# Layer 1 of a state-space kernel on Trainium2: three groups of 64 channels, two states to a unit

## The chip, the cores and the metric

The kernel runs on one core of one Trainium2 (trn2) chip. The engines of a core run side by side and meet through semaphores: TensorE (PE in the profile; PEld is its weight load), VectorE (DVE), ScalarE (ACT), GpSimd (POOL) and SyncE (SP), whose queue issues nearly all of the kernel's DMA transfers. The metric is the device time of one execution in microseconds (us); the median of several runs counts.

## What is computed

The input x has 64 x 64 tokens of 96 channels. Two Mamba-like layers are applied in turn, each behind a group norm and with its input added at the end. Layer 0 scans the picture in four directions. Layer 1, which the change is about, scans the 4096 tokens once, in order, with 192 inner channels d and 16 states n. Cut to what matters:

```python
xc = silu(causal depthwise conv of 3 taps over the x half of W_in u)   # 192 channels
dt, Bm, Cm = split(xc @ W_x)                                           # 6 + 16 + 16
delta = softplus(dt @ W_dt + b_dt)                                     # called dt in the kernel
dA = exp(delta[..., None] * A);  dBu = delta[..., None] * Bm[:, :, None, :] * xc[..., None]
def step(h, inp):
    h = dA_t * h + dBu_t
    return h, einsum('bdn,bn->bd', h, C_t)
y = scan(step) + xc * D
out = (y * silu(z)) @ W_out
```

So for each of 192 x 16 pairs of channel and state there is one recurrence over 4096 tokens, and the 16 states of a channel are summed with C as weights.

## The kernel before

Every engine operation is recorded through one helper (`Ordered`, line 377 in the profile), which also fixes the order on each engine as the order in which the program writes the instructions. A tile's name (y, f, C, dA) therefore tells an instruction apart, and its line does not.

**Layout.** Tokens are taken in four chunks of 1024 columns. The 128 partitions hold channels 0 to 127; the other 64 channels stand in columns 1024 to 1535 of tiles of 1536 columns, the first 512 tokens in partitions 0 to 63, the next 512 in 64 to 127 (`half1`, `part`). u, sz, dt and w (dt times u) have this form.

**Units.** A chunk has 24 units. In units 0 to 15 the partitions are the 128 low channels with one state n. In units 16 to 23 they are the 64 high channels twice, with states n and n + 8 (`UNITS`, line 36). For units 16 to 23 dt and w are needed on both halves of the partitions with all 1024 columns: `front_dup` (line 1444) copies them by DMA into tiles dt1 and w1 (pool "dup", two buffers), eight transfers of 128 KB a chunk. `of_unit` (line 1457) picks the source.

**One unit s** goes through these steps:

- `load`: SP loads row n of C, spread over the partitions (one DMA of 512 KB, or two of 256 KB where the unit has two states). There are six C buffers. For the units of `POOL_UNITS` (five in each chunk) B is loaded in the same way, into one buffer.
- `spread`: otherwise PE spreads B over the partitions, into the PSUM tile f (two buffers): a matmul with a picking matrix, on B split in bfloat16 parts (`front_b`).
- `decay`: ACT computes dA = exp(dt * A). For POOL's units it goes to an f buffer, and POOL multiplies B by w (`pool_f`).
- `scan`: DVE multiplies f by w and runs the recurrence into h (three buffers); ACT keeps the last column (`keep_last`).
- `times_c`: POOL multiplies C by h.
- `fold`: PE adds the product to y: for units 0 to 15 with the identity into y0 (128 output columns, two banks), for 16 to 23 with the matrix `both` into y1 (64 output columns for each half of the tokens, one bank). The skip term u * D enters by `skip` with diagonal weights.

A matmul in float32 is two records in the trace, so a fold is four.

**Order.** `run` (line 1804) writes the steps by hand: in step s it issues the shared work of the chunk (`between`), the loads of unit s + 3, the spread and POOL's decay for s + 1, ACT's decay for s + 2, the softplus pieces, the scan of s, the product with C of s - 1 and the fold of s - 2. `between` puts the next chunk's projections, the output of the chunk before (`back`) and z between the units. `soft` (line 1767) spreads the next chunk's softplus over the steps from 10 on (15 in chunk 0): Abs, two sigmoids, two squares in a step each, DVE's two products in a step each, w on POOL, the copies. After unit 20 `gate(c, 0)` multiplies y0 by sz; `gate(c, 1)` for y1 comes with the next chunk. `start` (line 1686) does the front of chunk 0 and `end` the output of chunk 3.

Of the kernel before, what the change touches and what calls it, by code (L numbers as in the profile page):

```python
# [20 lines left out]
C = 96  # L21
# [18 lines left out]
WHOLE = 4  # L40

# [68 lines left out]
def minus_exp(nc, sb, vec, name):  # L110

    a = sb.tile([P, NVEC - ALOG], F32, name=f"A_{name}")
    nc.scalar.activation(a, vec[:, ALOG:], AF.Exp)
    nc.vector.tensor_scalar(a, a, -1.0, None, ALU.mult)
    return a
# [19 lines left out]
def load_layer1(nc, sb, vec, w_z, w_x, dt_w, w_out):  # L135

    lay = {}
    lay["vec"] = sb.tile([P, NVEC], F32, name="vec_1")
    nc.sync.dma_start(lay["vec"], vec)
    lay["w_z"] = sb.tile([C, 2, P], F32, name="wz_1")  # L140
    nc.sync.dma_start(lay["w_z"], w_z)
    lay["dt_w"] = sb.tile([DT_ROW + R, 2, P], F32, name="dtw_1")
    nc.sync.dma_start(lay["dt_w"][DT_ROW:], dt_w)
    lay["w_x"], lay["w_out"] = [], []
    for t in range(2):
        raw = sb.tile([P, E], F32, name=f"w_x_raw{t}")
        w_o = sb.tile([P, C], F32, name=f"w_out{t}_1")
        for to, src in ((raw, w_x), (w_o, w_out)):
            if t == 0:
                nc.sync.dma_start(to, src[0:P])  # L150
            else:
                nc.sync.dma_start(to[0:HALF], src[P:DI])
                nc.sync.dma_start(to[HALF:P], src[P:DI])
        wx = sb.tile([P, ROWS], F32, name=f"w_x{t}_1")
        nc.gpsimd.memset(wx, 0.0)
        for copy in range(3):
            nc.gpsimd.tensor_copy(wx[:, 32 * copy : 32 * copy + NS], raw[:, R : R + NS])
        nc.gpsimd.tensor_copy(wx[:, DT_ROW : DT_ROW + R], raw[:, 0:R])
        nc.gpsimd.tensor_copy(wx[:, C_ROW : C_ROW + NS], raw[:, R + NS : E])
        lay["w_x"].append(wx)  # L160
        lay["w_out"].append(w_o)
    return lay
# [1107 lines left out]
class Layer1:  # L1270
# [6 lines left out]
    def __init__(self, nc, tc, st, k, lay, w_in, conv_w, x1, stats, bc_dram, out, g):  # L1277
# [39 lines left out]
        for n, b in (("f", 2), ("y0", 1), ("y1", 1), ("misc", 1)):  # L1317
            self.pools[n] = st.enter_context(
                tc.tile_pool(name=f"{n}_1{g}", bufs=b, space=PSUM)
            )  # L1320
# [38 lines left out]

    def conv_taps(self, xn):  # L1360
        return [(self.cw[:, j, :], xn[:, j : j + CH]) for j in range(3)]

    def z_taps(self, xn):
        return [(self.lay["w_z"].rearrange("c t p -> c (t p)"), xn[:, 2 : 2 + CH])]
# [24 lines left out]
    def front_z(self, c):  # L1389
        of, self.at = self.chunks[c], c  # L1390
        of["sz"] = sz = self.tile("uz", [P, CW], "sz")
        for q in range(3):
            ps = self.misc(c, [P, NB], f"pz{q}")
            yield from self.steps(self.product(ps, q, self.z_taps(of["xn"])))
            self.nc.scalar.copy(sz[:, self.part(q)], ps)
# [48 lines left out]
    def front_dup(self, c):  # L1444

        of = self.chunks[c]
        self.at = c
        of["dup"] = {}
        for name in ("dt", "w"):
            of["dup"][name] = to = self.tile("dup", [P, CH], f"{name}1")  # L1450
            for share in range(2):
                for hf in range(2):
                    self.nc.sync.dma_start(
                        to[self.half1(share), self.part(hf)], of[name][self.half1(hf), CH:CW]
                    )

    def of_unit(self, name, s):
        c, i = divmod(s, UNIT)
        of = self.chunks[c]
        return of[name][:, 0:CH] if i < NS else of["dup"][name]  # L1460
# [31 lines left out]
    def load(self, s):  # L1492
        self.at, of = s, self.units[s]
        c, i = divmod(s, UNIT)
        for part, name in enumerate("BC"):
            if part or self.on_pool(s):
                of[name] = self.tile(name, [P, CH], name)
                load_states(
                    self.nc, of[name], self.bc_dram[part], 0, (UNITS[0] + UNITS[1])[i], c
                )  # L1500
# [10 lines left out]
    def spread(self, s):  # L1511
        self.at = s
        c, i = divmod(s, UNIT)
        self.units[s]["f"] = f = self.tile("f", [P, CH], "f")
        for hf in range(2):
            if s < WHOLE:
                pick, of = free(self.k["ident"][0:B_ROWS, :], (0, P), at=i), "dbl"
            else:
                pick, of = self.k["pick"][:, i, :], "B"
            self.nc.tensor.matmul(  # L1520
                f[:, self.part(hf)], pick, self.chunks[c][of][0:B_ROWS, self.part(hf)],
                start=True, stop=True,
            )
# [24 lines left out]
    def skip(self, c, q):  # L1548

        of, self.at = self.chunks[c], c  # L1550
        if q == 0:
            of["y0"] = self.tile("y0", [P, CH], "y0")
        if q == 2:
            of["y1"] = self.tile("y1", [P, NB], "y1")
        self.nc.tensor.matmul(
            of["y1"] if q == 2 else of["y0"][:, self.part(q)], self.diag[:, q // 2, :],
            of["u"][:, self.part(q)], start=True, stop=False,
        )

    def fold(self, s):  # L1560
        nc, k, terms = self.nc, self.k, self.units[s]["C"]
        c, i = divmod(s, UNIT)
        of = self.chunks[c]
        for hf in range(2):
            if i == 0:
                self.skip(c, hf)
            if i < NS:
                nc.tensor.matmul(
                    of["y0"][:, self.part(hf)], k["fold"][0], terms[:, self.part(hf)],
                    start=False, stop=(i == NS - 1),  # L1570
                )
            else:
                nc.tensor.matmul(
                    of["y1"][self.half1(hf), :], k["fold"][1][:, 0:HALF], terms[:, self.part(hf)],
                    start=False, stop=(i == UNIT - 1),
                )


    def gate(self, c, t):
        of, col = self.chunks[c], (slice(0, CH), slice(CH, CW))[t]  # L1580
        self.at = c
        if t == 0:
            of["v"] = self.tile("v", [P, CW], "v")
        self.nc.vector.tensor_mul(of["v"][:, col], of[f"y{t}"], of["sz"][:, col])

    def out_products(self, c, hf, po):
# [3 lines left out]
            ((po, w, of), {"start": i == 0, "stop": i == 2})  # L1590
            for i, (w, of) in enumerate((
                (self.k["ident"][0:C, 0:C], self.x1[:, cols]), (w_out[0], v[:, self.part(hf)]),
                (w_out[1][half, :], v[half, CH:CW]),
# [29 lines left out]
    def end(self):  # L1623
# [3 lines left out]
        at = self.tile("y0", [P, 2, NB], "y0")  # L1627
        po = [at[0:C, hf] for hf in range(2)]
        products = [self.out_products(c, hf, po[hf]) for hf in range(2)]
        for part in products:  # L1630
            for args, kw in part[0:2]:
                nc.tensor.matmul(*args, **kw)
        yield
        self.gate(c, 1)
        for part in products:
            args, kw = part[2]
            nc.tensor.matmul(*args, **kw)
# [17 lines left out]
    def start(self):  # L1655
# [55 lines left out]
        self.front_w(0, (slice(0, CH),), nc.vector)  # L1711
# [3 lines left out]
        pz, pz1 = bank("y0", [P, 2, NB], "pz"), bank("y1", [P, NB], "pz1")  # L1715
        for q in range(2):
            do(self.product(pz[:, q], q, self.z_taps(xn)))
        do(self.product(pz1, 2, self.z_taps(xn)))
# [7 lines left out]
        for q in range(3):  # L1726
            nc.scalar.copy(sz[:, self.part(q)], pz[:, q] if q < 2 else pz1)
# [10 lines left out]
    def between(self, c):  # L1738

        more = c + 1 < NSC  # L1740
        if c == 0:
            yield from self.front_u(1)
        yield from self.silus(c)
# [4 lines left out]
        if c:  # L1748
            self.gate(c - 1, 1)
        self.skip(c, 2)  # L1750
# [19 lines left out]
    def soft(self, c):  # L1770

        def piece(c, col):
# [7 lines left out]
            for i in range(2):  # L1780
                soft_square(nc, k, q, i)
                yield
            soft_times(nc, acc, q)
            yield
            nc.vector.scalar_tensor_tensor(dt, dt, 0.0, acc, ALU.max, ALU.add)
            yield
            self.front_w(c, (col,), nc.gpsimd)
            yield
            self.front_dup(c)
# [4 lines left out]
        for i in range(UNIT):  # L1794
# [4 lines left out]
            next(done, None)  # L1799
            if i in ((18, 20, 21, 22) if c == 0 else (14, 16, 18, 20)):  # L1800
# [3 lines left out]
    def run(self):  # L1804
# [5 lines left out]
        for s in range(n + 2):  # L1810
# [27 lines left out]
            if i == NS + 4 and c < NSC:  # L1838
                self.gate(c, 0)
# [10 lines left out]
def tile_kernel(  # L1850
# [44 lines left out]
    def load(nc):  # L1895
# [4 lines left out]
        lay0["A"] = minus_exp(nc, const, lay0["vec"], "0")  # L1900
# [10 lines left out]
        lay1["A"] = minus_exp(nc, const, lay1["vec"], "1")  # L1911

        k["pick"] = pick = const.tile([B_ROWS, NS + NS // 2, P], BF16, name="pick")
# [3 lines left out]
        for first, n, at, cols in (  # L1917
            (0, NS, 0, slice(0, P)),
            (0, NS // 2, NS, slice(0, HALF)),
            (NS // 2, NS // 2, NS, slice(HALF, P)),  # L1920
        ):
            nc.gpsimd.tensor_copy(
                pick[:, at : at + n, cols],
                free(state, (1, n), (0, cols.stop - cols.start), at=first),
            )
# [85 lines left out]
```

## Time and profile before

| | us |
|---|---|
| median of 3 runs | 570.2 |
| lowest and highest | 567.95, 571.04 |
| the profiled execution | 571.18 |
| its span, first to last instruction | 569.4 |
| busy PE | 482.6 |
| busy DVE | 461.7 |
| busy POOL | 348.8 |
| busy ACT | 328.4 |

The span is what the profile's times refer to; the profiled execution's own time is 1.8 us longer and 1.0 us above the median. Busy times are sums over the whole span, and the span has stages with different limits: layer 0 to about 158 us, the front of layer 1 to 187, the 96 units to 555, the tail. The chain of work that ended last goes through PE for 24% of the span and through DVE for 23%. "x96" is a number of instructions, and a row "a <-b" says that b ended the wait of a. PE's ends are modelled, so in PE's timeline the distance from one start to the next is more certain than a duration.

### The profile page before, as it was taken

The page shows a single profiled execution, that of the slowest core. Times are in us where ns is not written, and L with a number is a line of the kernel's source. Part 1 is how long each engine was busy: PE and PEld are TensorE (multiplying, and loading weights), DVE is VectorE, ACT ScalarE, POOL GpSimd, SP SyncE. Part 2 cuts the span into 40 slices and gives each one's busy share as a digit, 9 for nine tenths or more (in the row PEclk, how much of TensorE's full clock was granted, in tenths as well). Part 3 has the DMA queues.
Part 4 walks back from the last instruction along what each step waited for, and adds up shares of the span by engine and source line. Part 5 has one row for each costly group of instructions (what it writes and reads, how often), then busy time and mean ns, then how long its engine had stood idle before and what let it go on. Part 6 is the DMA issues. An engine that isn't in the chain of part 4 may idle for free.

```text
span 569.4 us, 4766 instructions
## 1 busy us (share of the span) xinstructions
PE 482.6 (85%) x1363; PEld 195.3 (34%) x1363; DVE 461.7 (81%) x442; ACT 328.4 (58%) x486; POOL 348.8 (61%) x204
## 2 busy tenths in 40 slices
PE   4999999988889998996899978679976847986782
PEld 3545445436732333331133323113422202432220
DVE  6897989255733979998989979896978899899991
ACT  5437993478636876695856765464585454243300
POOL 7080010014320697989997859975886988789861
PEclk9996999997997999997599979779989767999778
DMA  6103800000003537786655649764648675677701
GB/s 170 21 9 72 281 2 0 0 1 1 2 28 113 155 130 222 214 202 154 192 195 188 207 94 224 201 187 126 199 142 198 149 184 184 199 238 190 191 22 35
DMA packets 30502, 75.76 MB, mean 133 GB/s; under 512 B 10880, under 2 KB 12156, under 8 KB 30210
## 3 DMA queue, kind: packets, MB, share of 16 engines
q1 hardware_dynamic: 29186, 73.83, 45.8%
q10 hardware_dynamic: 1280, 1.52, 0.9%
q8 instruction: 13, 0.21, 0.2%
q14 instruction: 23, 0.19, 0.1%
HBM read 68.93 MB, written 2.25 MB: 125 GB/s over the span
## 4 chain that ended last, share of the span: by engine, by line
PE 24%; DVE 23%; ACT 11%; POOL 5%; issue 4%; DMA 4%; SPq 1%; POOLq 0%; DVEq 0%; ACTq 0%
DVE h L377 15%; PE y L377 11%; DVE f L377 5%; PE f L377 3%; ACT q L377 3%; POOL C L377 2%; PE pd L377 2%; ACT dA L377 2%; PE po L377 2%; DMA C<-bc_dram 2%; ACT f L377 2%; SPq L377 1%; PE pc L377 1%; ACT L377 1%; PE pv L377 1%
## 5 line engine op out<-in xcount | busy, mean ns | idle before, releaser
L377 POOL TENSOR_TENSOR C<-C,h 128x1024 f32<-128x1024 f32 x96 | 229.5, 2403 | 51.4 <-issue 19.6
L377 DVE TENSOR_TENSOR_SCAN h<-dA,last,f 128x1024 f32<-128x1024 f32 x57 | 133.8, 2347 | 7.9 <-POOL C L377 0.5
L377 PE MATMUL y<-C,ident 128*128 128x512 f32 x256 | 130.5, 632 | 4.5 <-POOL C L377 4.3
L377 DVE TENSOR_TENSOR f<-f,w 128x1024 f32<-128x1024 f32 x76 | 92.4, 1215 | 16.8 <-PE f L377 16.2
L377 ACT ACTIVATE dA<-dt,A 128x1024 f32<-128x1024 f32 x76 | 86.3, 1143 | 2.2 <-DVE h L377 1.9
L377 PE MATMUL f<-parts,pick 96*128 96x512 bf16 x144 | 50.5, 437 | 35.6 <-DVE h L377 35.6
L377 PEld LDWEIGHTS y<-C,ident 128*128 128x128 f32 x256 | 50.9, 203 | 60.5 <-issue 43.1
L377 PE MATMUL pc<-pad,cw 96*128 96x512 f32 (+1 forms) x144 | 59.8, 576 | 0.8 <-ACT v L377 0.8
L377 PE MATMUL y<-C,both 128*64 128x512 f32 x128 | 44.2, 784 | 9.8 <-POOL C L377 9.8
L377 POOL TENSOR_TENSOR B<-B,w 128x1024 f32<-128x1024 f32 x20 | 47.1, 2354 | 7.2 <-DMA B<-bc_dram 7.2
L377 ACT COPY last<-h 128x1 f32<-128x1 f32 x72 | 13.5, 187 | 64.2 <-DVE h L377 64.1
L377 DVE TENSOR_TENSOR_SCAN h<-dA,f 128x1024 f32<-128x1024 f32 x19 | 43.4, 2287 | 2.4 <-POOL C L377 0.2
L377 PEld LDWEIGHTS <-pick 96*128 96x128 bf16 x144 | 10.9, 102 | 94.1 <-DVE h L377 47.1
L377 ACT ACTIVATE f<-dt,A 128x1024 f32<-128x1024 f32 x20 | 22.3, 1116 | 35.3 <-DVE h L377 26.9
L377 PEld LDWEIGHTS pc<-pad,cw 96*128 96x128 f32 x144 | 28.5, 200 | 32.0 <-issue 27.7
L377 ACT ACT_TABLE_LOAD x28 | 35.9, 1283 | 2.1 <-PEq L2001 1.7
L377 DVE TENSOR_TENSOR_SCAN h<-f,last,B 128x1024 f32<-128x1024 f32 x15 | 34.9, 2330 | 0.0
L377 PE MATMUL pc<-xn,cw 96*64 96x512 f32 (+1 forms) x84 | 29.9, 603 | 0.1
L377 POOL TENSOR_SCALAR ln_small<-ln_small 128x4 f32<-128x4 f32 x2 | 0.5, 235 | 42.5 <-DVE ln_small L377 42.5
L377 POOL TENSOR_TENSOR rest<-dbl,parts 96x1024 f32<-96x1024 f32 (+1 forms) x5 | 10.0, 2000 | 26.0 <-ACT parts L377 25.8
L377 POOL MEMSET wda<- 128x4 f32 (+3 forms) x8 | 0.9, 119 | 37.3 <-ACT wda L377 37.3
L377 PEld LDWEIGHTS y<-C,both 128*64 128x64 f32 x128 | 7.8, 161 | 31.7 <-POOL C L377 20.7
(212 smaller groups left out, 727.9 us busy)
## 6 DMA issues: line engine op xcount, KB each, us to landing
C<-bc_dram SPq DMA_DIRECT2D x64, 512.0 KB, 4.0
C<-bc_dram SPq DMA_DIRECT2D x64, 256.0 KB, 4.7
B<-bc_dram SPq DMA_DIRECT2D x12, 512.0 KB, 5.4
B<-bc_dram SPq DMA_DIRECT2D x16, 256.0 KB, 5.4
dt<-dt SPq DMA_DIRECT2D x16, 128.0 KB, 4.4
w<-w SPq DMA_DIRECT2D x16, 128.0 KB, 4.0
wB<-rows_dram SPq DMA_DIRECT2D x1, 1472.0 KB
wC<-rows_dram SPq DMA_DIRECT2D x1, 1472.0 KB
```

The lines of the kernel that those rows point to most:

```text
L377: ins = it(*args, **kw)
```

## The change

All 24 units of a chunk take the form that units 16 to 23 had. The 192 channels are three groups of 64; unit i of a chunk belongs to group i // 8 and holds states i % 8 and i % 8 + 8. There are three sums y0, y1 and y2 of one bank each. Every C and B load is now two DMAs of 256 KB. A is laid out by groups when the weights are loaded, with W_out in three pieces; the picking matrices are built for the pairs.

```diff
-    def front_dup(self, c):
+    def front_dup(self, c, g, parts=(slice(0, CH),)):
...
         for name in ("dt", "w"):
-            of["dup"][name] = to = self.tile("dup", [P, CH], f"{name}1")
             for share in range(2):
-                for hf in range(2):
-                    self.nc.sync.dma_start(
-                        to[self.half1(share), self.part(hf)], of[name][self.half1(hf), CH:CW]
-                    )
+                to = dup[name][self.half1(share)]
+                if g == 2:
+                    for hf in range(2):
+                        self.nc.sync.dma_start(
+                            to[:, self.part(hf)], of[name][self.half1(hf), CH:CW]
+                        )
+                else:
+                    for col in parts:
+                        self.nc.sync.dma_start(to[:, col], of[name][self.half1(g), col])

     def of_unit(self, name, s):
         c, i = divmod(s, UNIT)
-        of = self.chunks[c]
-        return of[name][:, 0:CH] if i < NS else of["dup"][name]
+        return self.chunks[c]["dup"][i // PAIRS][name]
...
     def fold(self, s):
...
+        g, n = divmod(i, PAIRS)
+        if i == 0:
+            self.skip(c, g)
+        for hf in range(2):
+            nc.tensor.matmul(
+                self.chunks[c][f"y{g}"][self.half1(hf), :], k["fold"][1][:, 0:HALF],
+                terms[:, self.part(hf)], start=False, stop=(n == PAIRS - 1),
+            )
```

In `out_products` the output is the sum of four products (the residual and three over 64 rows each) where it was three, and z and D are computed by pairs of products of 64 columns. In `start` the first w is made in halves, and dt and w are copied for group 0 before the first decay:

```diff
         for p in range(2):
             col = self.part(p)
             soft_vector(nc, dt[:, col], acc[:, col], sq[:, col])
-        self.front_w(0, (slice(0, CH),), nc.vector)
+            self.front_w(0, (col,), nc.vector)
+            self.front_dup(0, 0, (col,))
```

In `soft` the steps move, and the copies get places of their own:

```diff
             for i in range(2):
                 soft_square(nc, k, q, i)
-                yield
-            soft_times(nc, acc, q)
             yield
-            nc.vector.scalar_tensor_tensor(dt, dt, 0.0, acc, ALU.max, ALU.add)
+            yield
+            soft_vector(nc, dt, acc, q)
             yield
             self.front_w(c, (col,), nc.gpsimd)
-            yield
-            self.front_dup(c)
             yield
...
+            if i == 3:
+                self.front_dup(c, 1)
+            if i == 10:
+                self.front_dup(c, 2)
+            if c + 1 < NSC and i == (21 if c == 0 else 17):
+                self.front_dup(c + 1, 0)
```

Gates 0 and 1 of a chunk stand after units 20 and 21, gate 2 with the next chunk. The number of decays, spreads, scans and products with C, and their sizes, stay as they are; so do the pools in SBUF and POOL's units.

## The prediction

> **What bounds the kernel now.** I first cut the span by stages. Layer 1's 96 units (four chunks of 24) run from about 183 to 555 us, and the change touches little else. Busy time per engine in that stretch (us, instructions; columns PE, weight loads, DVE, ACT, POOL, then PE clock, DMA share, GB/s):
>
> ```profile
> 183.00:555.00 372.00, 312.98 (x781) 105.43 (x780) 333.12 (x192) 211.82 (x277) 305.94 (x134) 0.88 0.63 177
> ```
>
> DVE is busy 333 of 372 us. It does a product (1.2 us) and a scan (2.3 us) for most units, only the scan for the 20 units that POOL prepares. From its first product at 187.55 to the end of its last scan at 554.13 are 366.6 us. The change cannot shorten DVE's own work, so what it can win there is DVE's idle time. Second view, what DVE waits for:
>
> ```profile
> DVE f L377 <- PE f L377: 16.2, 12, 3.9
> DVE acc L377 <- ACT q L377: 10.4, 5, 3.8
> DVE v L377 <- PE y L377: 3.7, 1, 3.7
> DVE h L377 <- POOL C L377: 0.7, 2, 0.5
> DVE h L377 <- ACT f L377: 0.5, 1, 0.5
> ```
>
> 16.2 us are waits for B spread by PE. Of the 10.4 us for ACT's squares, 0.8 lies before the first scan; the 3.7 is in the tail. By DVE's timeline the idle between first product and last scan is 16.5 + 9.6 + 1.2 = 27 us. That is the ceiling.
>
> Third view, the sums ("folds") into y, four records a unit: with 128 output columns (ident) and with 64 (both):
>
> ```profile
> L377 PE MATMUL y<-C,ident 128*128 128x512 f32 x256 | 130.5, 632 | 4.5 <-POOL C L377 4.3
> L377 PE MATMUL y<-C,both 128*64 128x512 f32 x128 | 44.2, 784 | 9.8 <-POOL C L377 9.8
> ```
>
> The mean of one record misleads: 784 ns is more than 632, but the 64-column records run two at a time, so 32 units cost 44.2 us (1.38 each), and 64 wide units 130.5 (2.04 each). PE's timeline shows it at full clock (first four lines) and at half clock (last):
>
> ```profile
> 304.33 0.60 PE L377 MATMUL f<-parts,pick 96*128 96x512 bf16 x2
> 304.77 1.88 PE L377 MATMUL y<-C,ident 128*128 128x512 f32 x4
> ...
> 353.63 1.08 PE L377 MATMUL y<-C,both 128*64 128x512 f32 x4
> 354.64 0.55 PE L377 MATMUL pt<-ident,oc 96*128 96x96 f32 x4
> ...
> 264.47 1.98 PE L377 MATMUL y<-C,both 128*64 128x512 f32 x4
> 266.37 2.08 PE L377 MATMUL pz<-xn,wz 96*128 96x512 f32 x2
> ```
>
> From start to start a wide fold takes 1.72 us (304.77 to 306.49), a narrow one 1.01 (353.63 to 354.64), and 1.90 where the clock is 0.5.
>
> **Folds.** 64 units become narrow. PE time falls by 64 x (2.04 - 1.38) = 42 us by the means. Bounds: 64 x 0.71 = 45 us at full clock, and a loss of 64 x 0.18 = 12 us if every narrow fold met the half clock and every wide one the full. I take the means. Only what PE delays DVE counts. I went through the waits one by one:
> - Wide folds at full clock ahead of a spread: 1.05 (at 203), 0.2, 1.6 (298), 0.1, 3.9 (395), 0.1; sum 7.0. PE runs without a gap from 380 to 395: projections, four D and fold products, a fold, a D product, a dt product. Narrow pairs take 2 to 2.5 us out of that; 1.4 of the 7.0 stays.
> - Half clock: 0.8 (385), 1.1 (452, behind a wide fold of 3.6), 1.9 (490); sum 3.8, 1.5 stays.
> - A fold held by a late POOL product, with the spread behind it: 0.6 (354), 1.7 (370), 0.7 (467), and 0.2 (283); sum 3.1, 0.8 stays, since w moves (below).
> - ACT's copy of the output held PE at 423: 2.6; 2.2 stays, nothing there changes.
>
> 16.5 becomes 5.9: **-10.6 us** (bounds 0 and -16.5).
>
> A narrow product stands between wide spreads. The spread takes 0.44 us before a wide fold (304.33 to 304.77) and 0.53 before a narrow one in the same timeline (355.03 to 355.56), so a change of width costs about 0.1 there, inside what I took. The Trainium skill, page "TensorEngine Tiling (Array Packing)", section "Key Properties", speaks against the change: a change of tiling mode drains the engine. It gives up to 2x for columns of 64 or fewer; by that the fold would be 0.86, by the row 1.01, and the estimate of PE time saved 55 us instead of 45.
>
> A less busy PE may also be clocked lower. The row: after 4.2 us of idle at 259 to 263 the granted clock was 0.85, then 0.5 from 265 to 280, and narrow folds took 1.9 us. The skill's page "TensorE: Matmul & The Clock Gate", Part 1, says this is the rule: idle windows of about 3.4 us throttle to half, sustained work releases it. By that rule more folds than now would run at 1.9, and the gain would tend to the lower bound.
>
> **soft moved.** The second square is issued one step earlier, ahead of one or two decays; both softplus products come in one step; POOL's w one step earlier. ACT does the same work. The four waits 1.1, 2.6, 3.9, 2.0 lose what stood between: q at 208; f, dA (2.2 us) at 257; dA (1.1) at 330; copies and dA (1.5) at 428. Left: 0.1, 1.2 (0.4, but POOL has no gap from 259.8 to 289, so part comes back as a wait for POOL), 2.8, 0.5. **-5.0 us** (bounds 0 and -9.6). w (3.4 us on POOL) falls into a gap at 333 to 338 that POOL now idles; that is why its products are less late at 350 to 370.
>
> **Group copies.** dt and w are copied for all three groups: 12.6 MB instead of 4.2. What a copy costs:
>
> ```profile
> C<-bc_dram SPq DMA_DIRECT2D x64, 256.0 KB, 4.7
> B<-bc_dram SPq DMA_DIRECT2D x16, 256.0 KB, 5.4
> dt<-dt SPq DMA_DIRECT2D x16, 128.0 KB, 4.4
> w<-w SPq DMA_DIRECT2D x16, 128.0 KB, 4.0
> ```
>
> In SP's timeline four issues take 2.45 us, 0.6 each. SP gets 8 more copies, 16 more C and 2 to 3 more B issues a chunk: 27 x 0.6 = 16 us in a chunk of some 90. SP has room, it waits 207 us for folds to free C. Groups 1 and 2 are copied 3 and 4 steps (10 us and more) before the first decay that reads them, and need no wait for w; the next chunk's group 0 five steps before (one less in chunk 0), behind w. Behind each stand C loads, used four steps later, and B loads; the eight issues that stood ahead of a B load at unit 18 (B landed 1.2 and 2.6 late for POOL) become four. A 256 KB copy of this kind is not in the trace; between 1.6 us (a 32 KB write) and 5.4 (B), I take 4.5. I put **+2.0 us** for what isn't hidden (bounds 0 and 20).
>
> **The start is not hidden.** Now DVE goes straight from w to the first product:
>
> ```profile
> 186.22 1.22 DVE L377 TENSOR_TENSOR w<-dt,u 128x1024 f32<-128x1024 f32 x1
> 187.55 1.23 DVE L377 TENSOR_TENSOR f<-f,w 128x1024 f32<-128x1024 f32 x1
> 188.89 2.29 DVE L377 TENSOR_TENSOR_SCAN h<-dA,f 128x1024 f32<-128x1024 f32 x1
> ```
>
> After: dt and w of each half, then eight copies. First dt is ready at 184.0, eight issues at 0.6 end at 188.9; the last starts at 188.2 and lands 2 to 4.5 us later. At 3.3: first product at 191.5 instead of 187.55, **+4.0 us** (bounds +2.5 and +6). ACT's table load and decay wait for dt, which lands 1.2 earlier, and end in time. All the rest of layer 1 moves along.
>
> **Smaller.** Three gates of 512 columns (0.59 each) for one of 1024 (1.11) and one of 512: +0.3. The output takes three products over 64 rows for one over 128 and one over 64: about +1 us of PE for each half. Inside the chunks it is paid from the folds; in the tail the products after 550.9 stand ahead of the last two folds, so **+1.0** (bounds 0 and 2). z in pairs (1.08 for 1.05) and D likewise: nothing. Eight more small loads (5 us of SP) fall into SP's gap from 18.3 to 37.6; without it they'd delay the window stage by as much.
>
> **Sum** on the profiled execution (span 569.4, time 571.18): 571.2 - 10.6 - 5.0 + 2.0 + 4.0 + 0.3 + 1.0 = 562.9. It lies 1.0 over the median of 570.2, so I forecast **562**; own range 555 to 567.
>
> **Rivals.**
> 1. All of it works: idle 27 goes to nearly 0, start +2.5: 570.2 - 27 + 2.5 + 0.3 + 1 = 547 to 555. For it: the last stretch, 490 to 554, runs without any DVE idle, wide folds and all. Against: POOL without gaps, and ACT's row of table loads. Chance 0.10.
> 2. The clock takes it back (the narrow folds don't do what they say): folds at 1.9, PE waits fall by only 4, ACT's by 2: 570.2 - 6 + 2 + 4 + 1.3 = 571.5; 567 to 574. For it: clock 0.5 wherever PE is idle now. Against: half clock comes where PE has little to do. Chance 0.16.
> 3. Slower: DMA. Between 448 and 458, at a share over 1.0, the engines moved 221 to 238 GB/s; 8.4 MB more are 37 us of all 16 engines, and the share goes from 0.63 to about 0.74. B has one buffer, so its load can't start earlier, and POOL already waits up to 2.6 us for it. POOL idles 66 us, 3.3 for each of 20 B units. From 3.3 us more on a B landing, the rest is DVE's: at 4.5, 20 x 1.2 = 24 us: 561 + 24 = 585; 574 to 590. Against: B's neighbours on the queue become fewer where it is late now. Chance 0.19.
>
> The forecast has 0.55. About 0.5% (2.9 us) is what a measurement can tell from no change. Faster: forecast and rival 1, 0.65, and the low edge of rival 2, 0.01. Same: most of rival 2, 0.14. Slower: rival 3 and the high edge of rival 2, 0.20. The range takes in rival 2, the low end of rival 3 and most of rival 1: 550 to 577.
>
> **What would show it.** Right: y folds all "both", near 1.3 us a unit; DVE's waits for PE under 8 us, for ACT's squares under 6; the first scan 4 us later after w; POOL's wait for B not above 10 us. Wrong: clock under 0.8 between 185 and 555 with DVE still waiting 12 us or more for PE; decays that wait for copies; POOL waiting for B by 3 us each time; a first product later than 194.

## The result, and the profile after

| | before | after |
|---|---|---|
| median, us | 570.6 (567.95 to 571.37) | 590.5 (584.33 to 592.91) |
| profiled execution, us | 571.18 | 592.91 |
| its span, us | 569.4 | 590.8 |
| its mean granted clock of TensorE | 0.90 | 0.83 |

After is slower: ratio 1.034, 95% interval 1.025 to 1.043. In a second comparison it was 1.024 (1.016 to 1.032). The forecast was 562. (Executions over 1.5% above the fastest of their kernel are left out of a ratio; for one kernel below, rows_and_split, that left too few, and it has none.)

The changed kernel records every operation through line 388. Layer 1's stage, the same columns as in the prediction's first view (PE, weight loads, DVE, ACT, POOL; then PE clock, DMA share, GB/s):

```profile
190.00:575.00 385.00, 300.13 (x802) 69.25 (x802) 337.51 (x191) 210.49 (x274) 302.16 (x133) 0.77 0.80 188
```

PE is busy 300 us where it was 313, in a stretch 13 us longer, at a clock of 0.77 instead of 0.88. DVE's waits in this stage:

```profile
DVE f L388 <- PE f L388: 30.9, 15, 6.4
DVE f L388 <- DMA w<-w: 5.5, 1, 5.5
DVE acc L388 <- ACT q L388: 2.9, 1, 2.9
```

The waits for ACT's squares fell from 9.6 to 2.9 us. Those for PE, which were to fall to 5.9, rose from 16.2 to 30.9 (to 24.9 in the second trace of after, run after_again). Three groups of PE products:

```profile
L388 PE MATMUL y<-C,both 128*64 128x512 f32 x384 | 131.7, 774 | 18.6 <-POOL C L388 18.5
L388 PE MATMUL f<-parts,pick 96*128 96x512 bf16 x144 | 56.6, 483 | 39.9 <-DVE h L388 32.8
L388 PE MATMUL po<-v,w_out 64*96 64x512 f32 x36 | 23.7, 774 | 0.0
```

The folds cost 131.7 / 96 = 1.37 us a unit, just as priced: 43 us less than the 174.7 before. But the same 144 spreads went from 50.5 to 56.6, and other products rose too; in sum PE won 13 us, not 43. Where DVE waits longest, PE's timeline shows why:

```profile
407.09 1.98 PE L388 MATMUL y<-C,both 128*64 128x512 f32 x4
408.99 2.07 PE L388 MATMUL pv<-dbl,dtw 6*128 6x512 f32 x2
411.00 1.03 PE L388 MATMUL f<-parts,pick 96*128 96x512 bf16 x2
...
424.44 3.73 PE L388 MATMUL po<-v,w_out 64*96 64x512 f32 x4
428.10 1.03 PE L388 MATMUL f<-parts,pick 96*128 96x512 bf16 x2
```

The spread takes 1.0 us from start to start, a narrow fold 1.9: half clock, with no gap between 404.8 and 431.7. DVE's next product waited 6.4 us for the spread at 428.1.

The start, on DVE:

```profile
184.51 0.69 DVE L388 TENSOR_TENSOR w<-dt,u 128x512 f32<-128x512 f32 x1
190.71 1.23 DVE L388 TENSOR_TENSOR f<-f,w 128x1024 f32<-128x1024 f32 x1 [5.51 <-DMA w<-w]
192.06 2.29 DVE L388 TENSOR_TENSOR_SCAN h<-dA,f 128x1024 f32<-128x1024 f32 x1
```

And the transfers, with their time from issue to landing as the last number:

```profile
C<-bc_dram SPq DMA_DIRECT2D x192, 256.0 KB, 5.1
B<-bc_dram SPq DMA_DIRECT2D x40, 256.0 KB, 5.0
dt<-dt SPq DMA_DIRECT2D x14, 256.0 KB, 5.0
w<-w SPq DMA_DIRECT2D x14, 256.0 KB, 7.3
```

**Where the 21.7 us between the two profiled executions lie.** First DVE product: 190.71 against 187.55, +3.2 (layer 1's first projection started 1.7 earlier in this execution, at 162.6 instead of 164.3, so the start itself cost 4.9). From there to the end of the last scan: 384.4 against 366.6, +17.8, of which 9.8 is DVE's idle time and 8.1 its busy time. Tail: +0.4, and 0.3 more lies outside the span. That DVE would be busy longer was in no step of mine. It is this:

```profile
267.25 1.73 DVE L388 SCALAR_TENSOR_TENSOR acc<-q,acc 128x1536 f32<-128x1536 f32 x1
269.01 3.79 DVE L388 SCALAR_TENSOR_TENSOR dt<-dt,acc 128x1536 f32<-128x1536 f32 x1
```

Two softplus products of one size stand back to back, and the second takes 3.79 us instead of 1.73. POOL in the same moment:

```profile
267.46 3.72 POOL L388 TENSOR_TENSOR C<-C,h 128x1024 f32<-128x1024 f32 x1 [1.18 <-DVE h L388]
```

POOL's product, 2.37 us elsewhere, takes 3.72. The times fit if the two take turns (the trace does not show the turns themselves): POOL's stands until DVE's first product ends at 268.98, then takes 2.2 us to its end at 271.18, and DVE's second one then needs 1.6 us to its end at 272.80. The Trainium skill, page "GPSIMD Engine Reference", section "1. Specifications", says that POOL shares its SBUF interfaces with VectorE and contends with DVE instructions that have two SBUF inputs. The rows agree: the softplus products read two SBUF tiles, while scans (2.28 to 2.35 us) and f products (1.20 to 1.23), which read f from PSUM, keep their length beside POOL.

### The profile page after: what moved, and what is told of

It is laid out like the page before. It is cut to its first block, busy times and chain, and to the rows that moved or that the text cites. A ratio compares the mean times of both kernels' runs of the same rounds, so it can differ in the third digit from the quotient of the medians.

```text
span 590.8 us, 5150 instructions
## 1 busy us (share of the span) xinstructions
PE 477.9 (81%) x1411; PEld 160.9 (27%) x1411; DVE 468.1 (79%) x447; ACT 329.2 (56%) x486; POOL 345.0 (58%) x205
## 4 chain that ended last, share of the span: by engine, by line
PE 39%; DVE 25%; ACT 17%; DMA 6%; issue 6%; POOL 5%; SPq 2%; DVEq 0%; POOLq 0%; ACTq 0%
DVE h L388 15%; PE pc L388 8%; PE y L388 8%; DVE f L388 6%; PE po L388 5%; PE f L388 4%; DMA C<-bc_dram 3%; ACT L388 3%; ACT dA L388 3%; PE pz L388 2%; ACT q L388 2%; PE pw L388 2%; DMA dt<-dt 2%; ACT wg L388 2%; SPq L388 2%
## 5 line engine op out<-in xcount | busy, mean ns | idle before, releaser
L388 POOL TENSOR_TENSOR C<-C,h 128x1024 f32<-128x1024 f32 x96 | 227.2, 2381 | 55.9 <-DVE h L388 23.7
L388 PE MATMUL y<-C,both 128*64 128x512 f32 x384 | 131.7, 774 | 18.6 <-POOL C L388 18.5
L388 DVE TENSOR_TENSOR f<-f,w 128x1024 f32<-128x1024 f32 x76 | 92.3, 1214 | 36.4 <-PE f L388 30.9
L388 PE MATMUL f<-parts,pick 96*128 96x512 bf16 x144 | 56.6, 483 | 39.9 <-DVE h L388 32.8
L388 POOL TENSOR_TENSOR B<-B,w 128x1024 f32<-128x1024 f32 x20 | 47.4, 2368 | 17.4 <-DMA B<-bc_dram 11.7
L388 PEld LDWEIGHTS y<-C,both 128*64 128x64 f32 x384 | 23.5, 160 | 83.8 <-POOL C L388 42.4
L388 PE MATMUL pc<-xn,cw 96*64 96x512 f32 (+1 forms) x84 | 35.6, 671 | 6.9 <-ACT dt L388 6.2
L388 PEld LDWEIGHTS pc<-pad,cw 96*128 96x128 f32 x144 | 28.4, 200 | 32.0 <-issue 27.7
L388 POOL TENSOR_TENSOR rest<-dbl,parts 96x1024 f32<-96x1024 f32 (+1 forms) x5 | 8.7, 1735 | 32.2 <-ACT parts L388 32.1
L388 PE MATMUL po<-v,w_out 64*96 64x512 f32 x36 | 23.7, 774 | 0.0
L388 PE MATMUL pz<-xn,wz 96*64 96x512 f32 x36 | 13.8, 858 | 8.6 <-ACT sz L388 6.3
```

The lines of the kernel that those rows point to most:

```text
L388: ins = it(*args, **kw)
```

## The experiments

Theories. **Clock**: the saved PE time becomes gaps behind which PE works at half clock, so the saving is paid back; in the expectations also A or G (gaps alone, whatever the products are), B (narrow products do not bring the clock back) and W (the folds' form decides). **R**: products over few rows keep the clock low. **C**: the softplus products of DVE and the products of POOL exclude each other. **DMA**: rival 3 of the prediction. All ratios are to the kernel before, run beside each kernel on the same chip.

| run | edit | median us (lowest to highest) | ratio, 95% interval | clock of the profiled execution |
|---|---|---|---|---|
| after_again | after | 587.3 (577.8 to 591.8) | 1.024 (1.016 to 1.032) | 0.84 |
| split_soft | after, DVE's softplus in two steps | 586.3 (581.2 to 592.9) | 1.027 (1.022 to 1.033) | 0.82 |
| rows_full | after, full rows | 581.2 (580.6 to 586.0) | 1.024 (1.015 to 1.033) | 0.86 |
| rows_again | the same | 582.8 (579.8 to 586.7) | 1.025 (1.019 to 1.030) | 0.87 |
| rows_and_split | both | 579.8 (568.2 to 584.1) | none | 0.86 |
| combo | both, another order, two queues | 590.0 (581.6 to 591.1) | 1.031 (1.019 to 1.043) | 0.86 |
| wide_folds2 | after, all folds wide | 592.1 (591.2 to 594.8) | 1.042 (1.034 to 1.050) | 0.93 |
| after_folds_undone | after, folds of two groups wide | 591.5 (585.6 to 596.8) | 1.033 (1.026 to 1.040) | 0.90 |
| folds_alone | before, y0 folds narrow | 572.5 (570.0 to 578.8) | 1.009 (1.005 to 1.013) | 0.85 |
| folds_rows_full | the same, full rows | 571.6 (567.8 to 573.3) | 1.006 (1.002 to 1.009) | 0.87 |
| before_rows_full | before, full rows | 567.0 (564.4 to 575.6) | 0.998 (0.994 to 1.003) | 0.91 |
| soft_moved | before, after's softplus order | 570.2 (567.2 to 575.6) | 1.003 (0.998 to 1.007) | 0.91 |
| sq_early | before, second square early | 571.2 (565.5 to 576.1) | 1.003 (0.999 to 1.007) | 0.91 |
| before_more_dma | before, 8.4 MB more copies | 570.1 (567.0 to 574.7) | 1.004 (1.000 to 1.009) | 0.91 |
| fill_1 | before_rows_full and 20 zero products | 573.0 (569.0 to 579.9) | 1.006 (1.003 to 1.010) | 0.93 |
| fill_2 | the same with 40 | 577.7 (576.4 to 579.0) | 1.014 (1.010 to 1.018) | 0.94 |

### The transfers

before_more_dma loads every C and B row by two transfers and adds copies that nothing reads:

```diff
+    states = states * (2 // len(states))
...
+            if i in (2, 4, 19, 21):
+                self.more_copies(c, ("dt", "w")[i in (4, 21)], i < 5)
```

> The kernel before with the transfers of the changed one: every C and B load as two of 256 KB, and 8.4 MB of further copies of dt and w (16 of 256 KB each), which nobody reads. If the copies and loads by themselves cost the time (the prediction's third rival): 10 to 20 us slower than before, with POOL's wait for B over 20 us. If they are hidden, as I now think: within 4 us of before, since the changed kernel's POOL waited 11.7 us for B against 7.2.

Ratio 1.004: at most 5 us, most likely 2.5. POOL's waits for B stayed at 7.2 us. Rival 3 falls as the cause; my +2.0 for the copies fits.

### What keeps TensorE's clock up

clock: nine stretches of one kind of work each, about 11 us of waiting ahead of each.

> Measures PE's clock by kind of product and computes nothing of the layers: nine stretches of one kind of product each, back to back, each behind about 10 us in which PE waits for ACT. In the changed kernel PE worked without a gap from 404.8 to 431.8 us at a clock of 0.5, on products of 64 columns, of 64 or 6 rows and on spreads. Theory A (gaps): the clock falls in a gap and comes back after some 5 to 9 us of work of any kind. Then every stretch begins at half clock and goes to full within 10 us; narrow pairs go from 1.7 to 1.9 us a pair to 0.86, and the stretch with 6 rows shows the same. Theory B (kind of product): wide products bring the clock back, narrow ones or those over few rows do not; then the narrow, 64-row or 6-row stretches stay at 0.5 for 30 us and more, while the wide ones go to 1.0 within 10 us. In the mixed stretches (two spreads and a narrow pair; two spreads and two wide products) A expects full clock in both, B only in the wide one.

Windows inside six of the stretches: wide folds, narrow pairs, products over 64 rows, products over 6 rows, spreads alone, and steps of two spreads and a narrow pair.

```profile
20.00:50.00 30.00, 30.00 (x69) 13.21 (x68) 0.00 (x0) 0.00 (x0) 0.00 (x0) 1.00 0.00 0
70.00:100.00 30.00, 30.00 (x142) 9.82 (x140) 0.00 (x0) 0.00 (x0) 0.00 (x0) 1.00 0.00 1
120.00:180.00 60.00, 60.00 (x72) 19.42 (x71) 0.00 (x0) 0.00 (x0) 0.00 (x0) 0.50 0.00 0
200.00:265.00 65.00, 65.00 (x78) 24.89 (x77) 0.00 (x0) 0.00 (x0) 0.00 (x0) 0.50 0.00 0
285.00:330.00 45.00, 41.08 (x71) 7.35 (x70) 0.00 (x0) 0.00 (x0) 0.00 (x0) 0.50 0.00 0
360.00:390.00 30.00, 28.96 (x102) 5.18 (x100) 0.00 (x0) 0.00 (x0) 0.00 (x0) 1.00 0.00 1
```

B falls for the 64 columns: narrow pairs ran at full clock. But products over 64 rows, or over 6, worked 60 us and more without a gap and stayed at 0.5. After has more of them, three 64-row products for each half of the output instead of one. So theory R. Rows are not the whole rule: spreads alone, bfloat16 over 96 rows and busy 41 of 45 us, stayed at 0.5 as well, while the same spreads between narrow pairs ran at 1.0. What exactly brings the clock back is not shown.

rows_full pads them with zeros, as many products of the same length:

```diff
-        rows = slice(DT_ROW, DT_ROW + R)
+        rows = slice(0, DT_ROW + R)
...
-                *((w_out[g][half, :], v[half, self.part(g)]) for g in range(GROUPS)),
+                *((w_out[g][:, hf, :], v[:, self.part(g)]) for g in range(GROUPS)),
```

> The kernel after, with the same number of products of the same length, but all of po and pv over full rows: the three pieces of W_out per half are padded with 64 zero rows and taken over 128 rows, and the dt product takes 102 rows (zero weights but for six) instead of 6. Theory R (products over few rows don't bring the granted clock back, as the 69 us at 0.5 over 64 and over 6 rows in the run clock showed; after has more of them, three of 64 rows per half of po instead of one): the mean clock rises from 0.83-0.86 to 0.88 or more, DVE's waits for PE in the stage fall from 30.9 us to 18 or less, the time to 574-582 us. Theory G (the clock falls behind PE's gaps only, and what rows the next products have is no matter): nothing changes, 584-593 us and clock 0.83-0.86.

> The kernel before with the same padding as in the run rows_full: the second piece of W_out over 128 rows (64 zero) and the dt product over 102 rows instead of 6. Theory R: its stretches at half clock behind pv and po get shorter, waits for PE from 16 us to 8-12, ratio 0.985-0.995. If rows only matter where PE is short of full-row work, as in after: within 0.5% of before.

Waits for PE in rows_full:

```profile
DVE f L390 <- PE f L390: 21.0, 10, 4.1
```

The direction of R, but short of it: clock 0.86 where 0.88 was expected, waits 21.0 (19.7 in rows_again) where at most 18 were, and the ratio to the kernel before, 1.024, is inside the intervals of after. In before_rows_full the waits for PE fell from 16.2 to 12.2 us, the clock stayed at 0.91, and the ratio is 0.998. Side by side in one comparison, the medians of after_again and rows_again were 4.5 us apart, while their ratios agree; over all ten executions of each, the medians are 588.8 and 581.5. I take some 5 us for likely, not settled.

> The kernel after once more, unchanged, beside the three below: 584-593 us, ratio 1.025-1.043 as in the first comparison.

> After with full rows in po and pv, once more: 6-10 us under after in the same job (579-584 us) if the rows matter; within 3 us of it if the first comparison was chance.

### The folds alone

This is the term that failed, made in the kernel before and nothing else with it (half of y0's channel sums are left out, so this kernel's output is not the layer's):

```diff
-            if i < NS:
+            if i < NS - 1:
+                half = self.half1(hf)
+                nc.tensor.matmul(
+                    of["y0"][half, self.part(hf)], k["fold"][0][:, half], terms[:, self.part(hf)],
+                    start=False, stop=False,
+                )
+            elif i < NS:
```

> The kernel before with the folds alone changed: 15 of the 16 y0 folds of each chunk have 64 output columns, the two halves in a pair, as after has them (it leaves out the sums of the other 64 channels of each half; everything else, softplus, loads, copies, is before's). By the term of my prediction: PE saves about 0.65 us in 60 units, DVE's waits for PE fall by up to 10 us, 556-562 us, ratio 0.975-0.99. Theory clock (PE then has more gaps and comes out of them at a lower granted clock, so the saving is paid back): ratio 0.995-1.015, mean clock 0.85-0.89 instead of 0.90-0.92, waits for PE 14 us or more.

Ratio 1.009: 5 us lost where I had -10.6. By 209.7 us PE in folds_alone is ahead: the chunk's last projection product is behind it, and it waits for DVE. The gaps of the kernel before in this stretch (the bracket is the idle time ahead):

```profile
215.23 0.61 PE L377 MATMUL f<-parts,pick 96*128 96x512 bf16 x2 [0.36 <-DVE h L377]
...
219.34 0.61 PE L377 MATMUL f<-parts,pick 96*128 96x512 bf16 x2 [1.79 <-DVE h L377]
```

and of folds_alone:

```profile
213.72 1.03 PE L377 MATMUL f<-parts,pick 96*128 96x512 bf16 x2 [2.94 <-DVE h L377]
214.68 1.98 PE L377 MATMUL y<-C,ident 128*64 128x512 f32 x4
```

Behind 1.79 us the spread still takes 0.45 from start to start; behind 2.94 it takes 0.96. What follows, in windows of the kernel before

```profile
230.00:250.00 20.00, 20.00 (x53) 7.97 (x52) 19.11 (x11) 14.94 (x20) 17.41 (x8) 1.00 0.72 208
```

and of folds_alone:

```profile
230.00:250.00 20.00, 20.00 (x35) 3.42 (x34) 10.33 (x7) 7.10 (x12) 11.20 (x5) 0.50 0.37 114
```

PE is busy all 20 us in both. In the first it does 53 records at full clock and DVE is busy 19 us; in the second 35 records at half clock, and DVE starves: 10.3. In this one stretch of projections, in which PE must keep up, DVE lost 9 us. This trace is of the longest of ten executions, 578.8 us against a median of 572.5, so the 9 us are more than usual. The low clock is usual: 0.845 to 0.873 in the ten, where the kernel before has 0.894 to 0.935 in all its executions.

folds_rows_full has the same narrow folds with full rows:

> Both of the two kernels above together: narrow folds (64 of 128 channel sums of y0 left out in 15 of 16 units) and full rows. Theory R and clock: full rows give back what the narrow folds lost, so this one shows the forecast gain of the folds at least in part: ratio 0.975-0.99 and waits for PE at or under 10 us. If the narrow folds by themselves lower the clock, no matter what stands beside them: ratio 0.995 or more, like the folds alone.

Waits for PE 16.4, but the ratio is 1.006. The clock fell behind a gap of 2.94 us here too, and was back at 228 instead of 251:

```profile
228.43 2.16 PE L381 MATMUL pd<-u,w_x 128*118 128x512 f32 x4
232.49 1.02 PE L381 MATMUL pv<-dbl,dtw 102*128 102x512 f32 x2
```

In folds_alone the same pd product took 4.04 us, from 227.55. The first padded product, pv over 102 rows, came only at 232.5, so the earlier return in this stretch is not the work of the full rows. With or without them, the narrow folds win nothing.

Is it the folds inside after, too? after_folds_undone puts the first two groups' folds, and the skip products, back to 128 columns by zero weights (wide_folds2 all three groups' folds):

```diff
-                self.chunks[c][f"y{g}"][self.half1(hf), :], k["fold"][1][:, 0:HALF],
-                terms[:, self.part(hf)], start=False, stop=(n == PAIRS - 1),
+                self.chunks[c][f"y{g}"], k["fold_wide"][:, (1 - hf) * HALF : (3 - hf) * HALF],
+                terms[:, self.part(hf)], start=False, stop=(n == PAIRS - 1 and hf == 1),
```

> The kernel after, with each of its narrow products (folds and skips, 64 output columns) made 128 columns wide by zero weights for the other half: the same sums in the same banks and at the same places, but the two of a pair one after the other, 1.7 us a unit of PE instead of 1.37 (0.86 us each in the profile of before). Theory W (the pairs of narrow products fill less of PE's time with work that brings the clock back): clock 0.88 or more, DVE's waits for PE at or under 22 us, 575-584 us although PE has some 30 us more to do. Theory G/R (the folds' form is no matter to the clock): PE has more to do at the same clock, its waits rise by 5 us or more, 592-600 us.

> After, with the folds of the first two groups 128 columns wide again (zero weights for the other half), so that PE has the work of before; the third group's stay narrow, everything else is after's. Theory clock (the narrow folds cost more by the lower clock than they save, 5 us in the run folds_alone): the clock comes back to 0.89 or more and the time to 579-586 us, 3-8 us under after. If the narrow folds save what the prediction said and something else in after lowers the clock: PE has 28 us more to do at the low clock, 595-605 us.

The clock came back (0.93 and 0.90) and the time did not: 592.1 and 591.5, no better than after. The stage of after_folds_undone, and DVE's waits in it:

```profile
190.00:575.00 385.00, 316.66 (x804) 105.64 (x804) 333.94 (x191) 211.27 (x274) 302.46 (x133) 0.88 0.80 189
DVE f L388 <- PE f L388: 28.4, 15, 5.3
```

The clock is that of the kernel before, 0.88, and PE does 317 us of work where it did 313; yet DVE waits 28.4 us for PE instead of 16.2 (25.9 in wide_folds2). So the lower clock of the narrow folds explains why they saved nothing, but not why PE is later in after than in the kernel before. Both sides of theory clock hold only in part: PE's work is less with narrow folds, its clock is lower, and the two cancel, somewhat to the worse in the kernel before (+5 us), somewhat to the better in after (some 4 us, the intervals overlap). A higher clock bought with more work buys nothing here. fill_1 and fill_2 say the same from another side: they add products with zero weights behind a fold wherever the next unit needs no spread.

> The kernel before with full rows (567.0 us in the run before_rows_full), and in each of the 20 steps whose next unit has its product on POOL (so that TensorE has no spread to do) one wide product with zero weights behind the fold, 0.43-0.86 us of TensorE at full clock each. If TensorE's gaps set its clock and the clock the time: mean clock 0.92-0.95, 562-566 us. If added work is only work: 568-575 us.

> The same with two such products in each of the 20 steps. Theory clock: 0.93-0.97, within 3 us of fill_1, on either side (1.7 us a step is about what the gaps hold). If added work is only work: 572-585 us.

Clock 0.91, 0.93, 0.94 and time 567.0, 573.0, 577.7: the clock rises and so does the time. In fill_2 DVE waits longer for PE than in the kernel before:

```profile
DVE f L381 <- PE f L381: 24.8, 16, 4.6
```

That expectation of mine was wrong. Added work is work.

### The gap and the pace

gaps measures both by itself: gaps of growing length between gapless wide products, then steps paced by ACT.

> Computes nothing of the layers. First, wide products without a gap (about 10 us or more each time), and between them ten gaps of about 1 to 5.5 us. Then TensorE paced by ACT, 20 steps each: two spreads and either two wide folds or a pair of narrow folds, one step per 3.5 us and then per 4.3 us, each after a gapless stretch at full clock. Theory clock: short gaps leave the clock at 1.0, and from some gap between 1.8 and 4 us on the next product runs at 0.5; at the kernel's pace (3.5 us) the wide steps hold 1.0 and the narrow ones (1.77 us of work at full clock, so gaps of 1.8 us) fall to 0.5-0.75. Rival (the clock falls with the share of idle time and not with a single gap): gaps of every size lower it in proportion, and the wide steps at 4.3 us fall like the narrow ones at 3.5 us.

```profile
169.78 1.13 PE L377 MATMUL acc_gap<-xt,key 128*128 128x512 f32 x2 [2.40 <-ACT key L377]
170.74 19.90 PE L377 MATMUL acc_gap<-xt,ident 128*128 128x512 f32 x46
193.48 2.08 PE L377 MATMUL acc_gap<-xt,key 128*128 128x512 f32 x2 [2.83 <-ACT key L377]
195.35 20.44 PE L377 MATMUL acc_gap<-xt,ident 128*128 128x512 f32 x46
```

After every gap up to 2.40 us the first product (two records) took 1.13 us; after 2.83 and after 4.11 it took 2.08, and after 3.26 the half clock came one product later. Some 3 to 5 us of wide work brought the full clock back, by the 1.5 to 2.7 us that these stretches took longer than the others. The Trainium skill, page "TensorE: Matmul & The Clock Gate", Part 1, puts the idle window at about 3.4 us; here 2.83 was enough. The paced steps, in windows: wide at one step per 2.96 us, narrow at the same, wide at one per 3.60, narrow at the same.

```profile
291.00:342.00 51.00, 41.42 (x109) 15.73 (x107) 0.00 (x0) 51.00 (x35) 0.00 (x0) 1.00 0.00 0
366.00:420.00 54.00, 36.23 (x116) 6.24 (x114) 0.00 (x0) 52.96 (x36) 0.00 (x0) 0.86 0.00 0
448.00:511.00 63.00, 40.44 (x106) 14.98 (x105) 0.00 (x0) 62.66 (x36) 0.00 (x0) 1.00 0.00 0
543.00:602.00 59.00, 48.46 (x102) 7.13 (x100) 0.00 (x0) 56.96 (x32) 0.00 (x0) 0.50 0.00 0
```

At 3.60 us a step, which is DVE's own pace (a product and a scan, 3.6 us), wide steps hold the full clock and narrow ones run at half for the whole 59 us. A wide step of that stretch, and the fall of the narrow ones:

```profile
453.13 0.61 PE L377 MATMUL f<-xb,key_wide 96*128 96x512 bf16 x2 [1.27 <-ACT key_wide L377]
453.57 1.88 PE L377 MATMUL acc_wide<-xt,ident 128*128 128x512 f32 x4
...
538.83 0.61 PE L377 MATMUL f<-xb,key_narrow 96*128 96x512 bf16 x2 [1.98 <-ACT key_narrow L377]
539.37 1.08 PE L377 MATMUL acc_narrow<-xt,both 128*64 128x512 f32 x4
542.43 1.03 PE L377 MATMUL f<-xb,key_narrow 96*128 96x512 bf16 x2 [1.98 <-ACT key_narrow L377]
543.39 1.98 PE L377 MATMUL acc_narrow<-xt,both 128*64 128x512 f32 x4
```

Each step is 3.60 us less its gap: 2.33 wide, 1.62 narrow at full clock, and 3.60 - 0.66 = 2.94 narrow at half. At this pace the "shorter" step is the longer one. Single gaps of 1.98 us, below the 2.40 that did no harm alone, were enough when they came in every step. The rival in its plain form (the clock falls in proportion to idle time) does not fit: wide steps at 3.60 idle 35% of the time at clock 1.0. A limit on the idle share is not excluded: the wide steps with gaps of 1.27 us idle 35% of their time and held 1.0, narrow ones at 2.96 us, with gaps of 1.34 at full clock, idle 45% and swung (0.86), narrow ones at 3.60 idled 55% and fell. Nor does this run tell the gap from the form of the product, since wide steps with gaps of 1.98 us were not run.

### The softplus order

soft_moved gives the kernel before the whole order of after; sq_early only the second square; split_soft puts DVE's two products in after a step apart again:

```diff
-            soft_vector(nc, dt, acc, q)
+            soft_times(nc, acc, q)
+            yield
+            nc.vector.scalar_tensor_tensor(dt, dt, 0.0, acc, ALU.max, ALU.add)
```

> The kernel before, with only the second square of the softplus on ACT one step earlier (in the first one's step), as after has it; the two DVE products stay a step apart. My term for it in the prediction: 5 us fewer waits of DVE for ACT squares (10.8 to about 5), 563-567 us, ratio 0.987-0.994. If the wait only goes to the next instruction (PE or POOL late instead), within 0.5% of before.

> The kernel before, with the whole order of after's softplus: both squares in one step, both products on DVE back to back in one step, w a step earlier. Theory C (the second product waits for POOL's product, since the two don't run together; 3.8 us instead of 1.73): the ACT waits fall by 5 us or more, but DVE's busy time in the stage rises by 5 to 8 us, and the time stays within 0.5% of before, 568-573 us. As I priced it in the prediction (no such cost): 563-567 us, like the kernel with the square alone.

> The changed kernel with DVE's two softplus products in a step each again, and w one step later, as before; the second square stays one step earlier. Theory C: the second product of a pair waits on DVE until POOL's product has ended (3.79 us instead of 1.73, three times, and 4.56 for 1.27 once). Then the three long ones go back to 1.73 and the 4.56 to under 2, DVE's busy time falls by 6 to 8 us, and the time by as much, to about 583. Rival (the waits only move to the first product or to POOL's w, which comes a step later and makes the copies late): under 2 us.

In soft_moved DVE's large softplus products

```profile
L377 DVE SCALAR_TENSOR_TENSOR acc<-q,acc 128x1536 f32<-128x1536 f32 x3 | 9.8, 3254 | 3.7 <-ACT q L377 3.7
L377 DVE SCALAR_TENSOR_TENSOR dt<-dt,acc 128x1536 f32<-128x1536 f32 x3 | 7.3, 2441 | 0.1
```

cost 17.1 us where the kernel before has 7.1 + 5.2 = 12.3; with the 512-column ones the rise is 7.8. ACT's waits in the stage fall from 9.6 to 3.7. Net +1.9, and the ratio is 1.003. Even sq_early, which moves no DVE product, had 5.3 us more of them: DVE meets POOL at another moment. So a square issued earlier moves the wait into DVE's busy time, and C holds. In after, split_soft ended the back-to-back cases (the second product 2.09 us on average, not 3.79), and the median fell by 1 to 4 us, inside the spread. One long product stayed, against the expectation: a first one of 512 columns beside a run of POOL products, 4.56 us in after and in split_soft where the kernel before has 1.27.

### Adding up

combo took full rows, the split and the eight copies at the start from two queues:

> After with what the runs so far showed to cost: full rows in po and pv (9 us in the run rows_full), the two softplus products of DVE a step apart again (about 4 us in split_soft), and the eight copies ahead of the first product issued by two queues, half by SP and half by ACT (SP's eight issues took 5.0 us; the first product some 2 us earlier). If the three add up: 573-577 us, ratio 1.005-1.015; if what is left of DVE's waits is of one kind (PE's clock), at or over 578 us.

590.0, a miss, and partly by my own edit: I had dropped an empty step, and DVE waited 15.9 us for the squares. The two queues did not help either: the first product still waited 6.3 us for w. rows_and_split keeps the step and one queue:

> After with full rows and with the two softplus products of DVE a step apart, with an empty step kept ahead of them (the run combo had left that step out, and DVE waited 15.9 us for the squares). If the two gains add: 3-4 us under rows_again, 575-580 us. If the POOL product in the way of DVE is only met elsewhere: the same as rows_again.

579.8, 3 us under rows_again, inside the spread of both. That is the best form of after, and 1.7% slower than before by the medians. No kernel here beats the one before by more than the uncertainty; before_rows_full is equal to it.

## Why the prediction was wrong, step by step

- **Folds, -10.6: the step that failed.** "I take the means" was right for the fold itself (1.37 us a unit) and wrong for the rest: I went through PE's waits and took a part out of each, as if all other products kept their speed. I had given the PE time a lower bound with a loss ("if every narrow fold met the half clock"), but the waits only "0 and -16.5". Alone the folds cost 5 us instead of saving 10.6: PE's gaps grew, the clock fell from 0.91 to 0.85, and the products behind ran at half speed (35 records in 20 us instead of 53). In after the waits for PE rose by 14.7 in the profiled execution, and since they stay at 28.4 with wide folds at the clock of before, most of this rise has other causes. Part of it are the 64-row products (21.0 with full rows) and the start (below); the rest is open. Rival 2 named the mechanism and was priced too kindly, at 571.5: it too let only the folds lose, not the spreads, projections and outputs behind them.
- **soft, -5.0: right waits, missed cost.** The waits fell by 6.7 us. DVE's softplus products grew by 7.7 in all: the three second ones now stood back to back with the first and met POOL's product (+6.2), one first product of 512 columns took 4.56 instead of 1.27 (+3.3), and the other first ones got shorter (-1.8). Net about +1, against +1.5 by soft_moved (not told from nothing). I had the first hint in the kernel before, a first product of 2.36 us on average beside a second one of 1.73, and did not ask what it waited for.
- **Start, +4.0: 4.9.** The last of the eight issues ended at 187.3, and w landed for the product at 190.7. Inside the bounds. The term missed one thing: PE idled 6.2 us behind the start as well, its next four records took 3.78 us (pc, at 193.69) instead of 1.88, and DVE waited 3.0 us at 200.9 for a spread (2.9 in after_folds_undone). These 3.0 are part of the 30.9.
- **Copies, +2.0: about 2.5** by before_more_dma. w's 256 KB copy landed in 7.3 us, more than my 4.5; behind the start DVE never waited for a copy, and one decay waited 2.8 us for dt's, at 286.7. POOL's wait for B was 11.7, slightly over the 10 I had named.
- **Gates and tail, +1.3: 0.4 for the tail, 0.5 for the gates.** Close.
- **The output products.** I let the folds pay the third product over 64 rows. They did not: these products went from 13.6 to 23.7 us, and part of that is clock.

Of the single effects, 5 (folds), 1.5 (softplus), 2.5 (transfers), 4.9 (start) and 0.7 (tail and the time outside the span) make 14.6 of the 17 to 20 us. What is left has the size of the gain from full rows. That the effects add is an assumption, and the 5 for the folds is from the kernel before: inside after, narrow folds came out some 4 us better than wide ones. Open is also why wide folds inside after do not give back the 5 us that narrow folds cost in the kernel before.

The signs I had named did their work: clock under 0.8 (0.77) and waits for PE over 12 us (30.9) both came.

## What to carry to other kernels

Time saved on an engine that waits for another becomes gaps; on TensorE, price the step at the clock that it will have at the pace of the engine it waits for, not at the clock it has now. Then look for the stretch in which TensorE must catch up, and read its clock there. A high clock is no aim either: products added to hold it cost more than they brought.

When an operation is moved next to another on DVE, look at what POOL does in that moment: a wait may only change into a longer instruction, which no list of waits shows.

## What the runs showed of the hardware

- A single gap of 2.40 us left TensorE's clock at 1.0, one of 2.83 did not. Narrow steps of 3.60 us with gaps of 1.98 fell to 0.5 and stayed there for the 59 us measured; wide steps of 3.60 with gaps of 1.27 held 1.0.
- Products over 64 rows, or over 6, ran at 0.5 for 60 us without a gap, and bfloat16 spreads over 96 rows at 0.5 for 45 us, busy 41 of them; narrow pairs over 128 rows ran at 1.0.
- Two products on DVE with both inputs in SBUF and one on POOL held each other up: 3.79 us instead of 1.73 for the second one on DVE, 3.72 instead of 2.37 on POOL.
